# A fused macaron block: its opening in another order, and its last sum in halves

## The chip, the cores and the metric

The kernel runs on one core of a Trainium2 chip. The metric is the device time of one execution in microseconds. Three runs of the kernel before gave 1027.17, 1028.06 and 1028.55 us, median 1028.06 us.

## The reference: what is computed

For x of 8 sequences by 1024 tokens by 128 features, all in float32, three residual steps follow each other:

```python
x = x + 0.5 * _L0_ffn_ref(_layernorm(x, axis=-1), ...)
x = x + _L0_attn_ref(_layernorm(x, axis=-1), L0_attn_w_q, L0_attn_w_k, L0_attn_w_v)
x = x + 0.5 * _L0_ffn_ref(_layernorm(x, axis=-1), ...)
```

The attention is causal, with one head of 128 and rotary positions. The feed-forward step is a mixture of 16 experts of inner width 64, of which a router picks 4 for each token, and one shared expert:

```python
scores = jax.nn.sigmoid(xt.astype(jnp.float32) @ gate_w.T)
_, idx = lax.top_k(scores + gate_b, TOPK)
w = jnp.take_along_axis(scores, idx, axis=-1)
w = w / jnp.sum(w, axis=-1, keepdims=True) * ROUTE_SCALE
comb = zeros.at[token, idx].add(w)
y = sum over experts e of comb[:, e] * (silu_and_mul(xt @ w13[e].T) @ w2[e].T)
y = y + silu_and_mul(xt @ w13_s.T) @ w2_s.T
```

So the router's weight of a token and an expert (`comb`) multiplies that expert's hidden values or its output. It isn't needed for the first product, `xt @ w13[e].T`.

## The kernel before, in words

**Groups.** A group is 512 tokens of one sequence in one of the two feed-forward layers: 2 layers by 8 sequences by 2 halves make 32 groups, in an order written out by hand (the first four sequences' first layer, then the two layers in turn). All 16 experts are computed for every token, as 8 pairs of 128 hidden units, and `comb` zeroes what wasn't picked.

**A group's steps** (class `Group`, L164 to L289). `norm_a` makes the reciprocal deviations: an addition on DVE (L147) and a power on POOL (L148). `norm_b` makes four normalised tiles on DVE (L155). `turn` transposes them on PE (L164) and copies them to `hT` on ACT (L165). `route` is four small products with the router's weights (L188), `score` an exponential on ACT (L194), `top_a`, `top_b` and `top_c` pick the four experts on DVE and make `comb` (L198 to L226). `spread` transposes `comb` on PE (L235), copies it on ACT (L237), writes it to DRAM (`cd`, L239) and reads it back in four DMAs, 512 KB each, so that every partition holds the weights of its expert (`cb`, L245). `up_shared` is the shared expert's product (L254 to L257). `up(k)`, for k from 0 to 7, is the main part: two products of 512 columns on PE (gate L264, up L265), a silu on ACT (L267), the product of the two on DVE (`hidT`, L269) and the multiplication by `cb` on POOL (L270). `down(k)`, for k from 0 to 8, sums the outputs in one bank of PSUM (L276); after k = 8 DVE copies the sum (L279). `add`, run in a slot of the next group, transposes it back (L284), adds it to x on DVE (L287) and for the second layer sends it out (L289).

**What sets the order.** The program is written in the order in which every engine takes its instructions. A group has 18 slots, U0 to U8 around its `up` steps and D0 to D8 around its `down` steps. A table `jobs` says which steps of other groups, of attention and of layer norm statistics stand in which slot; `run(p, slot)` emits them. Products `up(k)` use PSUM banks 2(k%2) and 2(k%2)+1, so an L265 needs the `hidT` product (L269) of two steps earlier to have been read out of its bank.

**The opening.** Group 0 has nobody in front of it. Before its first `up_shared` all its steps from `norm_a` to `spread` stand in one row; then come the statistics of the second half of sequence 0, and on the SP queue the loads of the first half of sequence 1, of the attention's weights, of the rotary table (1 MB), and of the second half of sequence 1. Group 1's `norm_a` stands in slot U1 of group 0, `norm_b` in U2, `turn` in U5, `route` in U6, `score` to `top_c` in D0 to D3, `spread` in D4. In `up(k)` the multiplication by `cb` is emitted right after the product on DVE, so on POOL it stands ahead of what the slot behind it brings, for k = 0 ahead of group 1's L148.

**The queues at the start.** SP's queue loads x (two halves of sequence 0), then the down weights `wd` (512 KB) and `wsd`; ACT's queue loads the router's weights, the shared expert's `ws` and the two halves of the gate and up weights (`wg`, `wu`, 256 KB each). Some of these issues wait for an earlier DMA that used the same semaphore.

Of the kernel before, what the change touches and what calls it, by code (L numbers as in the profile page):

```python
# [11 lines left out]
ALU = mybir.AluOpType  # L12
# [3 lines left out]
P = 128  # L16
# [10 lines left out]
def kernel(  # L27
# [14 lines left out]
    nc = tc.nc  # L42
# [4 lines left out]
    NT = S // P  # L47
    GT = 4
    NG = NT // GT
    W = GT * P  # L50
# [17 lines left out]
    def bank(i, n=1):  # L68
        return psum[:, i * W : (i + n) * W]
# [3 lines left out]
    def other_bank():  # L73
        spare[0] += 1
        return bank(6 + spare[0] % 2)

    def tiles_of(ap):
        return ap.rearrange("p (j q) -> p j q", q=P)

    ident = const.tile([P, P], F32, name="ident")  # L80
# [14 lines left out]
    xs, mvs = [None] * B, {}  # L95

    def load_x(b, g):
        if g == 0:
            xs[b] = xpool.tile([P, NT, D], F32, tag="x", name=f"x{b}")
        tiles = slice(g * GT, (g + 1) * GT)  # L100
        nc.sync.dma_start(
            out=xs[b][:, tiles, :], in_=x[b].rearrange("(t p) d -> p t d", p=P)[:, tiles, :]
        )
# [10 lines left out]
    for n in range(2):  # L114
        cols = slice(n * EI // 2, (n + 1) * EI // 2)
        nc.scalar.dma_start(out=wg[:, cols], in_=w_gate[:, cols])
        nc.scalar.dma_start(out=wu[:, cols], in_=w_up[:, cols])
    load_x(0, 1)
    wd = const.tile([P, NP, D], F32, name="wd")
    nc.sync.dma_start(out=wd, in_=w_down.rearrange("(n p) d -> p n d", p=P))  # L120

# [7 lines left out]
        shared.append(sh)  # L129
    wqkv = const.tile([P, 3, D], F32, name="wqkv")  # L130
    cs = const.tile([P, 2, S], F32, name="cs")

    def stats(key, b, tiles):

        if key not in mvs:
            mvs[key] = small.tile([P, NT, 2], F32, tag="mv", name=f"mv_{key}", bufs=16)
        for t in tiles:
            st = small.tile([P, 6], F32, tag="st", name=f"st_{key}_{t}")  # L140
            nc.vector.bn_stats(st, xs[b][:, t, :])
            nc.vector.bn_aggr(mvs[key][:, t, :], st)
# [26 lines left out]
    class Group:  # L169
# [89 lines left out]
        def up(self, k):  # L259

            nm = f"{self.nm}_{k}"
            units = slice(k * P, (k + 1) * P)
            g_ps, u_ps = bank(2 * (k % 2) + 1), bank(2 * (k % 2))
            nc.tensor.matmul(g_ps, wg[:, units], self.hT, start=True, stop=True)  # L264
            nc.tensor.matmul(u_ps, wu[:, units], self.hT, start=True, stop=True)  # L265
            sg = work.tile([P, W], F32, tag="sg", name=f"sg_{nm}")
            nc.scalar.activation(sg, g_ps, AF.Silu)  # L267
            hid = self.hidT[:, k, :]
            nc.vector.tensor_tensor(hid, u_ps, sg, ALU.mult)  # L269
            nc.gpsimd.tensor_tensor(hid, hid, self.cb[:, k, :], ALU.mult)  # L270

        def down(self, k):
            if k == 0:
                self.y = bank(0)
            w, h = (wd[:, k, :], self.hidT[:, k, :]) if k < NP else (wsd, self.sh)
            nc.tensor.matmul(self.y, w, h, start=(k == 0), stop=(k == NP))  # L276
            if k == NP:
                self.yT = work.tile([P, W], F32, tag="yT", name=f"yT_{self.nm}", bufs=2)
                nc.vector.tensor_copy(self.yT, self.y)  # L279

        def add(self):
            yp = tiles_of(other_bank())
            for j in range(GT):
                nc.tensor.transpose(yp[:, j, :], self.yT[:, j * P : (j + 1) * P], ident)  # L284
            tiles = slice(self.g * GT, (self.g + 1) * GT)
            xg = xs[self.b][:, tiles, :]
            nc.vector.scalar_tensor_tensor(xg, yp, 0.5, xg, ALU.mult, ALU.add)  # L287
            if self.layer == 1:
                nc.sync.dma_start(  # L289
                    out=out[self.b].rearrange("(t p) d -> p t d", p=P)[:, tiles, :], in_=xg  # L290
                )
# [115 lines left out]
    order = [(0, b) for b in range(LAG)]  # L407
    for b in range(LAG, B):
        order += [(1, b - LAG), (0, b)]
    order += [(1, b) for b in range(B - LAG, B)]  # L410
    groups = [
        Group(layer, b, g, 2 * n + g) for n, (layer, b) in enumerate(order) for g in range(NG)
    ]
    NPER = len(groups)
    heads = [Heads(b) for b in range(B)]

    jobs = {}

    def at(p, slot, *fs):
        jobs.setdefault((p, slot), []).extend(fs)  # L420
# [3 lines left out]
    def when(p, slot):  # L424
        return p * len(slots) + slots.index(slot)
# [4 lines left out]
    queue = [(b, i) for b in range(B) for i in range(NT)]  # L430
    starts, done = {}, {}
    for p in range(3, 29):
        for n in range(2 if p in (15, 21) or (p % 2 == 0 and p != 26) else 3):
            if not queue:
# [4 lines left out]
            s, first, e, t0, t1, a = (  # L439
                ((p, "U7"), 4, (p, "D0"), (p, "D3"), (p, "D5"), (p, "D7")),  # L440
                ((p, "D2"), 2, (p, "D5"), (p, "D8"), (p + 1, "U0"), (p + 1, "U2")),
                ((p, "D4"), 4, (p, "D7"), (p + 1, "U3"), (p + 1, "U4"), (p + 1, "U5")),
            )[n]
# [10 lines left out]
    for b in range(B):  # L454
        h, st = heads[b], starts[b]
        ready = when(turn_of[0, b, 1] + 1, "U7")
        if b == 0:
            p0, p1 = st - 1, st - 1
            places = ("U8", "D0", "D2", "D3", "D5", "D6", "D7", "D8")
        else:  # L460
            p0, p1 = st - 2, st - 1
            places = ("D0", "D3", "D5", "D8", "U1", "U3", "U4", "U6")
# [14 lines left out]
    for p, gr in enumerate(groups):  # L477
        steps = (
            gr.norm_a, gr.norm_b, gr.turn, gr.route, gr.score, gr.top_a, gr.top_b, gr.top_c,
            gr.spread,  # L480
        )
        if p == 1:
            places = [(0, s) for s in ("U1", "U2", "U5", "U6", "D0", "D1", "D2", "D3", "D4")]
        else:
            places = [(p - 2, s) for s in ("U5", "D1", "D4", "D6", "D7", "D8", "D8")]
            places += [(p - 1, "U1"), (p - 1, "U3")]
        if p > 0:
            for f, place in zip(steps, places):
                at(*place, f)
        if gr.layer == 1:  # L490
            for t in range(gr.g * GT, (gr.g + 1) * GT):
                assert done[gr.b, t] < when(p - 2, "U5")

        at(p + 1, "U3", gr.add)
        if gr.layer == 0:
            t = gr.g * GT
            for s in ("U5", "U7"):
                at(p + 1, s, lambda b=gr.b, t=t: stats(f"a{b}", b, (t, t + 1)))
                t += 2


    for b in range(2, B):
        p = turn_of[0, b, 0]
        for g in range(NG):
# [2 lines left out]
                p + g - 3, "D6",  # L507
                lambda b=b, g=g: stats(f"f0_{b}", b, range(g * GT, (g + 1) * GT)),
            )
    at(0, "U4", lambda: stats("f0_1", 1, range(GT)))  # L510
    at(0, "D6", lambda: stats("f0_1", 1, range(GT, NT)))

    def load_attention():
        nc.sync.dma_start(out=wqkv, in_=w_qkv)
        nc.sync.dma_start(out=cs, in_=rope)

    def run(p, slot):
        for f in jobs.pop((p, slot), []):
            f()

    gr = groups[0]
# [6 lines left out]
    gr.top_a()  # L528
    gr.top_b()
    gr.top_c()  # L530
    gr.spread()
    stats("f0_0", 0, range(GT, NT))
    load_x(1, 0)
    load_attention()
    load_x(1, 1)
    for p, gr in enumerate(groups):
        gr.up_shared()
        run(p, "U0")
        for k in range(NP):
            gr.up(k)  # L540
            run(p, f"U{k + 1}")
        for k in range(NP + 1):
            gr.down(k)
            run(p, f"D{k}")
    for p in (NPER, NPER + 1):
        for slot in slots:
# [73 lines left out]
```

## Time and profile before

| what | value |
|---|---|
| median of three runs | 1028.06 us |
| the profiled execution's own time | 1027.84 us |
| its span, first to last instruction | 1025.7 us |
| PE, matmuls | 993.1 us busy, 97% of the span |
| DVE / ACT / POOL | 662.5 / 419.7 / 451.9 us busy |
| DMA | 80.20 MB, 78 GB/s on average |
| mean granted PE clock in the records | 0.997 |
| first transpose on PE starts at | 7.42 us |
| first `up` product starts at | 17.14 us |
| last product of group 31 ends at | 1019.26 us |

The chain of waits goes back from the last instruction to the first: at each step to what released it, or to the instruction before it on the same engine. Its columns are the start, the length (both in us) and what it was. The timeline has start, length, engine, line, operation, output and inputs, and in brackets the idle time of the engine ahead of it with what ended it. The table by stage gives busy time of each engine, then the granted PE clock (1.00 is full), the share of DMA engines that were busy, and GB/s. One product in float32 shows as two instructions, so "x2" of L264, L265 or L276 is one product.

### The profile page before, as it was taken

To read this page: it belongs to the slowest core of one execution; us is meant where nothing else is said; L and a number is where in the kernel's file an instruction comes from. 1 tells how busy PE (TensorE), PEld (TensorE's weight loads), DVE (VectorE), ACT (ScalarE), POOL (GpSimd) and SP (SyncE) were. 2 spreads that over 40 slices of the span, in tenths; PEclk is the share of its full clock that TensorE was granted. 3 is DMA by queue.
4 is the path that set the end of the run, shared out by engine and by line. 5 is a ranking of instruction groups with operands and counts; after the bars stand their busy time and mean duration, and the time that the engine had idled before them with its cause. 6 is when DMAs were issued, how large, how long until landed. Compare 5 with 4: busy or idle time off the path is not lost.

```text
span 1025.7 us, 11327 instructions
## 1 busy us (share of the span) xinstructions
PE 993.1 (97%) x3520; PEld 534.2 (52%) x3520; DVE 662.5 (65%) x2032; ACT 419.7 (41%) x734; POOL 451.9 (44%) x382
## 2 busy tenths in 40 slices
PE   5799999999999999999999999999999999999997
PEld 2344455554555455545555555555565555555543
DVE  3566877667775776667677665776657757665542
ACT  2233544443534454434444444443444444343321
POOL 1445734265425562345524464334643355322433
PEclk9999999999999999999999999999999999999999
DMA  5485431354214530345213451234412343124440
GB/s 143 110 173 105 84 67 32 69 104 84 46 39 94 115 81 6 81 94 114 61 23 84 94 114 43 43 82 94 94 42 57 69 94 83 48 58 94 94 93 21
DMA packets 56748, 80.20 MB, mean 78 GB/s; under 512 B 3504, under 2 KB 23280, under 8 KB 56560
## 3 DMA queue, kind: packets, MB, share of 16 engines
q1 hardware_dynamic: 55680, 78.36, 35.5%
q10 hardware_dynamic: 1008, 1.13, 0.3%
q8 instruction: 27, 0.44, 0.2%
q14 instruction: 33, 0.27, 0.1%
HBM read 74.24 MB, written 5.24 MB: 77 GB/s over the span
## 4 chain that ended last, share of the span: by engine, by line
PE 86%; DVE 7%; DMA 2%; issue 2%; ACT 2%; POOL 0%; SPq 0%; ACTq 0%; POOLq 0%; DVEq 0%
PE psum L276 23%; PE psum L265 18%; PE psum L264 17%; PE psum L356 6%; PE psum L395 6%; PE psum L383 3%; PE psum L323 3%; PE psum L188 3%; PE psum L164 2%; PE psum L254 2%; DVE hidT L269 1%; DMA cb<-cd 1%; PE psum L337 1%; DVE sel L220 1%; PE psum L284 1%
## 5 line engine op out<-in xcount | busy, mean ns | idle before, releaser
L270 POOL TENSOR_TENSOR hidT<-hidT,cb 128x512 f32<-128x512 f32 x256 | 324.0, 1270 | 545.2 <-DVE hidT L269 497.3
L265 PE MATMUL psum<-hT,wu 128*128 128x512 f32 x512 | 263.2, 596 | 4.4 <-DVE hidT L269 4.4
L264 PE MATMUL psum<-hT,wg 128*128 128x512 f32 x512 | 263.4, 596 | 0.0
L267 ACT ACTIVATE sg<-psum 128x512 f32<-128x512 f32 x256 | 152.7, 597 | 233.0 <-PE psum L264 217.5
L276 PE MATMUL psum<-hidT,wd 128*128 128x512 f32 x512 | 248.0, 598 | 0.0
L269 DVE TENSOR_TENSOR hidT<-psum,sg 128x512 f32<-128x512 f32 x256 | 175.2, 686 | 100.5 <-PE psum L265 98.4
L265 PEld LDWEIGHTS psum<-hT,wu 128*128 128x128 f32 x512 | 97.7, 191 | 128.2 <-issue 104.2
L276 PEld LDWEIGHTS psum<-hidT,wd 128*128 128x128 f32 x512 | 89.2, 191 | 69.0 <-issue 62.7
L264 PEld LDWEIGHTS psum<-hT,wg 128*128 128x128 f32 x512 | 89.4, 193 | 65.8 <-issue 62.8
L387 ACT COPY prT<-psum 128x512 f32<-128x512 f32 (+2 forms) x64 | 32.4, 506 | 158.6 <-PE psum L383 158.6
L395 PEld LDWEIGHTS psum<-v,prT 128*128 128x128 f32 x576 | 74.4, 192 | 30.6 <-issue 26.5
L395 PE MATMUL psum<-v,prT 128*128 128x128 f32 x576 | 74.6, 275 | 0.0
L356 PE MATMUL psum<-k,q 128*128 128x512 f32 (+2 forms) x192 | 72.4, 486 | 0.0
L399 DVE SCALAR_TENSOR_TENSOR x<-psum,rl,x 128x128 f32<-128x128 f32 x64 | 22.1, 346 | 77.1 <-PE psum L395 70.0
L155 DVE TENSOR_SCALAR xn_f<-x,mv_f,rs_f 128x128 f32<-128x128 f32 x128 | 65.6, 573 | 5.8 <-POOL rs_f L148 5.7
L383 PEld LDWEIGHTS psum<-ident,pr 128*128 128x128 f32 x288 | 36.8, 141 | 49.9 <-issue 42.9
L356 PEld LDWEIGHTS psum<-k,q 128*128 128x128 f32 x192 | 36.6, 190 | 45.8 <-issue 45.1
L362 DVE TENSOR_REDUCE top<-psum 128x1 f32<-128x128 f32 (+3 forms) x64 | 48.5, 758 | 2.2
L383 PE MATMUL psum<-ident,pr 128*128 128x128 f32 x288 | 47.4, 274 | 1.9 <-DVE x L287 1.9
L367 ACT ACTIVATE pr<-psum,top 128x128 f32<-128x128 f32 (+3 forms) x64 | 47.3, 743 | 0.3
L360 DVE TENSOR_TENSOR psum<-psum,causal 128x128 f32<-128x128 f32 x64 | 19.0, 296 | 42.4 <-PE psum L356 42.0
L256 ACT ACT_TABLE_LOAD x31 | 39.8, 1283 | 10.2 <-PE psum L254 10.1
(77 smaller groups left out, 1013.6 us busy)
## 6 DMA issues: line engine op xcount, KB each, us to landing
cb<-cd SPq DMA_DIRECT2D x128, 512.0 KB, 8.5
x<-in_x SPq DMA_DIRECT2D x16, 256.0 KB, 10.9
out_x<-x SPq DMA_DIRECT2D x16, 256.0 KB, 2.4
cd<-cT SPq DMA_DIRECT2D x32, 32.0 KB, 1.8
cs<-in_rope SPq DMA_DIRECT2D x1, 1024.0 KB, 12.4
wd<-in_w_down SPq DMA_DIRECT2D x1, 512.0 KB, 8.1
wg<-in_w_gate ACTq DMA_DIRECT2D x2, 256.0 KB, 7.5
wu<-in_w_up ACTq DMA_DIRECT2D x2, 256.0 KB, 6.4
```

What stands on the lines that cost most here:

```text
L155: nc.vector.tensor_scalar(xn[:, j, :], xs[b][:, t, :], mvs[key][:, t, 0:1], rstd[:, j : j + 1], ALU.subtract, ALU.mult,)
L264: nc.tensor.matmul(g_ps, wg[:, units], self.hT, start=True, stop=True)
L265: nc.tensor.matmul(u_ps, wu[:, units], self.hT, start=True, stop=True)
L267: nc.scalar.activation(sg, g_ps, AF.Silu)
L269: nc.vector.tensor_tensor(hid, u_ps, sg, ALU.mult)
L270: nc.gpsimd.tensor_tensor(hid, hid, self.cb[:, k, :], ALU.mult)
L276: nc.tensor.matmul(self.y, w, h, start=(k == 0), stop=(k == NP))
L356: nc.tensor.matmul(s[:, c:e], h.q[:, i * P : width], h.k[:, c:e], start=True, stop=True)
L362: nc.vector.tensor_reduce(top, s[:, :width], AX.X, ALU.max)
L367: nc.scalar.activation(self.pr[:, : self.width], self.s[:, : self.width], AF.Exp, bias=self.top, scale=SCALE, accum_out=self.h.rl[:, self. ...
L383: nc.tensor.transpose(tp[:, j, :], self.pr[:, (k + j) * P : (k + j + 1) * P], ident)
L395: nc.tensor.matmul(o, self.prT[:, j, :], self.h.v[:, j, :], start=(j == 0), stop=(j == i))
```

## The change

Seven edits, all in the order of emission, in the first group or in the last:

1. Twelve products of the identity with itself, 128 by 128, are put on PE ahead of everything else; their result is overwritten.
2. `load_x(1, 0)`, 256 KB, moves on the SP queue from behind group 0's `spread` to the front of `wd`.
3. Group 0's `spread` moves from ahead of `up_shared` to slot U2, behind `up(1)`. `load_x(1, 1)`, the attention's loads and the statistics of the second half of sequence 0 follow it there; `load_x(1, 1)` now stands ahead of the attention's loads.
4. The multiplication by `cb` becomes a method of its own, `weigh(k)`. It stays where it was, save in group 0: `weigh(0)` is emitted behind `spread` in U2, and `weigh(1)` behind the jobs of U2.
5. Group 1's steps in group 0 move: `norm_a` U1 to U2, `norm_b` U2 to U3, `turn` U5 to U6, `route` U6 to U7, `spread` D4 to D6.
6. Group 2's `norm_a` moves from U5 to U8 of group 0, and the statistics of the first half of sequence 1 from U4 to U7.
7. Group 31's `down` copies its sum in two halves of 256 columns, the first on ACT and the second on DVE, and its `add` becomes `add_last`: two transposes, one addition and one output DMA for each half, the first DMA from ACT's queue, the second from SP's.

On the engines' queues this gives: PE takes the identity products, group 0's transposes and router products, `ws`, `up(0)`, `up(1)`, then the transpose of `comb`. POOL takes `weigh(0)`, then group 1's L148, then `weigh(1)`. DVE takes the choice of experts, then the shared product, the `hidT` products of 0 and 1, the statistics, the L147 addition, `hidT` of 2, the four tiles of `norm_b`, `hidT` of 3. The DMA of `wd` waits for the router's weights to land, which it didn't before. On DVE the second half's copy in group 31 waits for ACT's copy of the first.

```diff
     load_x(0, 1)
+    load_x(1, 0)
     wd = const.tile([P, NP, D], F32, name="wd")
...
+    for n in range(12):
+        nc.tensor.matmul(bank(2)[:, :P], ident, ident, start=True, stop=True)
...
             nc.vector.tensor_tensor(hid, u_ps, sg, ALU.mult)
+
+        def weigh(self, k):
+            hid = self.hidT[:, k, :]
             nc.gpsimd.tensor_tensor(hid, hid, self.cb[:, k, :], ALU.mult)
...
-                nc.vector.tensor_copy(self.yT, self.y)
+                if self.n == NPER - 1:
+                    H = W // 2
+                    nc.scalar.copy(self.yT[:, :H], self.y[:, :H])
+                    nc.vector.tensor_copy(self.yT[:, H:], self.y[:, H:])
+                else:
+                    nc.vector.tensor_copy(self.yT, self.y)
+
+        def add_last(self):
+
+            H = GT // 2
+            for n, queue in enumerate((nc.scalar, nc.sync)):
+                yp = tiles_of(other_bank())[:, :H, :]
+                t = self.g * GT + n * H
+                for j in range(H):
+                    k = n * H + j
+                    nc.tensor.transpose(yp[:, j, :], self.yT[:, k * P : (k + 1) * P], ident)
+                xg = xs[self.b][:, t : t + H, :]
+                nc.vector.scalar_tensor_tensor(xg, yp, 0.5, xg, ALU.mult, ALU.add)
+                queue.dma_start(
+                    out=out[self.b].rearrange("(t p) d -> p t d", p=P)[:, t : t + H, :], in_=xg
+                )
 
         def add(self):
+            if self.n == NPER - 1:
+                return self.add_last()
...
         if p == 1:
-            places = [(0, s) for s in ("U1", "U2", "U5", "U6", "D0", "D1", "D2", "D3", "D4")]
+            places = [(0, s) for s in ("U2", "U3", "U6", "U7", "D0", "D1", "D2", "D3", "D6")]
+        elif p == 2:
+            places = [(0, s) for s in ("U8", "D1", "D4", "D6", "D7", "D8", "D8")]
+            places += [(p - 1, "U1"), (p - 1, "U3")]
...
-    at(0, "U4", lambda: stats("f0_1", 1, range(GT)))
+    at(0, "U7", lambda: stats("f0_1", 1, range(GT)))
...
-    gr.spread()
-    stats("f0_0", 0, range(GT, NT))
-    load_x(1, 0)
-    load_attention()
-    load_x(1, 1)
+
+    jobs[0, "U2"] = [
+        gr.spread, lambda: load_x(1, 1), load_attention,
+        lambda: gr0.weigh(0), lambda: stats("f0_0", 0, range(GT, NT)),
+    ] + jobs.get((0, "U2"), [])
+    gr0 = gr
     for p, gr in enumerate(groups):
         gr.up_shared()
         run(p, "U0")
         for k in range(NP):
             gr.up(k)
-            run(p, f"U{k + 1}")
+            if p == 0 and k < 2:
+                run(p, f"U{k + 1}")
+                if k == 1:
+                    gr.weigh(k)
+            else:
+                gr.weigh(k)
+                run(p, f"U{k + 1}")
```

More of the change, by code (lines that the diff above doesn't have):

```diff
@@ L410 @@
     order += [(1, b) for b in range(B - LAG, B)]
+    NPER = NG * len(order)
     groups = [
@@ L413 @@
     ]
-    NPER = len(groups)
     heads = [Heads(b) for b in range(B)]
```

## The prediction, made blind

> **What bounds the kernel now.** I read the page first: the busy shares, the 40 slices and the chain's summary.
>
> ```profile
> span 1025.7 us, 11327 instructions
> PE 993.1 (97%) x3520; PEld 534.2 (52%) x3520; DVE 662.5 (65%) x2032; ACT 419.7 (41%) x734; POOL 451.9 (44%) x382
> PE   5799999999999999999999999999999999999997
> PE 86%; DVE 7%; DMA 2%; issue 2%; ACT 2%; POOL 0%; SPq 0%; ACTq 0%; POOLq 0%; DVEq 0%
> ```
>
> PE is full in every slice but the first two and the last. The edits touch only these, so a microsecond won in the first group is handed on by a stream that PE sets. Next, the chain in order of time, 0 to 60 us:
>
> ```profile
> 15.96 1.78 DMA cd<-cT
> ...
> 18.44 6.84 DMA cb<-cd
> ...
> 25.45 1.27 POOL hidT L270
> 26.71 0.98 POOL rs_f L148
> ...
> 28.92 0.85 DVE xn_f L155 x3
> 29.76 0.61 DVE hidT L269
> 30.37 0.04 issue
> 30.42 1.83 PE psum L265 x2
> ```
>
> PE stands still from about 26.7 to 30.42. The reason isn't that it lacks `cb`: POOL's first multiplication waits for `cb`, group 1's L148 is queued behind it, DVE's four tiles of `norm_b` (L155) wait for L148, the third `hidT` product is queued behind them, and PE's fifth L265 needs that product's bank. The timeline shows a second stop, 2.29 us, for `comb` of group 1, and what happens when POOL has work in store while DVE runs the four tiles:
>
> ```profile
> 46.29 0.30 PE L235 MATMUL psum<-ident,comb 128*64 128x128 f32 x1 [2.29 <-DVE comb L226]
> ...
> 124.31 3.73 POOL L270 TENSOR_TENSOR hidT<-hidT,cb 128x512 f32<-128x512 f32 x3
> 124.47 3.91 DVE L155 TENSOR_SCALAR xn_f<-x,mv_f,rs_f 128x128 f32<-128x128 f32 x4
> ```
>
> The same four tiles take 1.11 us at 7.02 where POOL is idle, 2.05 us at 27.72 beside one multiplication, and 3.91 us here beside three. The table by stage shows PE's clock:
>
> ```profile
> 20.46:30.70 10.24, 6.51 (x16) 2.76 (x15) 4.44 (x9) 2.39 (x4) 3.73 (x4) 1.00 1.09 223
> 30.70:34.10 3.40, 3.40 (x8) 1.77 (x8) 2.48 (x11) 0.58 (x1) 2.95 (x3) 0.50 0.97 366
> ```
>
> After the stop the clock is half for 3.4 us. Records begin at 20.46, yet the products between 15.4 and 20.46 start 1.71 us apart (17.14, 18.85) and later ones 0.86 (21.37, 22.23): PE starts at half speed too. Last, the chain's end:
>
> ```profile
> 1019.29 0.70 DVE yT L279
> ...
> 1020.03 0.67 PE psum L284 x4
> ...
> 1020.73 0.69 DVE x L287
> ```
>
> [...] raised 5.2 us after PE's steady work began (15.22 to 20.46), dropped at 30.70, raised again 3.4 us later. [...]
>
> **The change, part by part.**
>
> *Identity products.* Not in the trace; nearest are plain 128-column products at 0.107 us per instruction (L395: 6% of the span by 576 instructions), so 0.213 at half clock: 12 x 2 x 0.213 = 5.1 us from about 1.45 (the identity is ready at 1.40) to 6.6, ahead of the first transpose at 7.42. They cost nothing there; below nothing only through the clock. [...] I take a raised clock.
>
> *Up to `comb`.* At full clock the last transpose ends 0.2 us sooner (8.66 to 8.45), and the eight router instructions take 0.96 (row of 35.22) and not 1.89: `score` starts at 10.09 for 11.27, `comb` is done 1.18 sooner at 13.99. Meanwhile PE does what was behind it: five products (`ws`, two pairs) of 0.86, from 9.90 to 14.20. So `comb` is transposed at 14.20 and not 15.22; behind ACT's silu of pair 1 the copy ends at 14.80, and `cd` starts at 14.82 for 15.96: 1.14 sooner.
>
> *Weights.* Now `ws` is needed at 9.9, the first `wg` at 10.8, `wu` at 11.6. They landed at 8.8, 9.7 and 10.3 (issue plus landing in the DMA list). The 256 KB put in front lie on SP's queue, which was full of `wd` until 9.9 anyway; `wd` goes later, needed after 37. I take nothing; if the margin of 1.1 us breaks, up to 1 us of a PE that has to stop anyway.
>
> *The first stop.* With `cd` 1.14 sooner, `weigh(0)` runs at 24.31, L148 ends at 26.54. The knot is the same: L148 is still behind `weigh(0)`, and the move to U3 puts one more `hidT` in front of `norm_b`. PE therefore gets one pair further (through the sixth L264, at 20.6) and stops at the sixth L265. But now `weigh(1)` and `weigh(2)` are both ready, so two of the four tiles wait for POOL: the first ends at 27.86, the second 1.22 later, the others at 29.6; `hidT` 3 at 30.2. PE resumes at 30.25 for 30.42: the 1.14 is almost eaten by the second wait. The gain is the pair's 2 products: left over are five products, a set of transposes and the router, 5 x 0.86 + 0.43 + 0.80 = 5.5 us, plus 1.9 for the half clock (3.4 to 3.9 us of it) = 7.4[...]. The first `down` starts at 37.8 for 39.55: 1.75.
>
> *The second stop.* The chain to `comb` of group 1 runs from the last silu over the 1.28 us table load to `score`, then waits for POOL's last multiplication. All shift by about 1.8: `comb` at 44.4 for 46.24, group 2's tiles at 42.6 for 44.4. L148 of group 2, now behind `weigh(7)`, ends at 41.05, before its tiles start at 41.45. PE reaches these transposes after five `down` products (37.8 + 4.3 = 42.1): stops 0.5. It reaches `comb` after two more, 44.75: no stop. So 0.5 for 2.3, about 2.0 with the pipelines' overlaps (47.4 for 51.20 at the next `up_shared`, 3.8 in all). The statistics moved to U7 (1.6 us) end before the last `hidT` can start (37.8); POOL's backlog in group 1, with `cb` 2.2 us later against that group, is worked off before its `down` (weigh 5 at 63.3 for a need at 67). Cover gone, it would cost 0.3.
>
> *The end.* ACT's half copy 0.37 and DVE's 0.42 (rows of 128x256 below), in a row since DVE waits for ACT; two transposes 0.40; the half addition about 0.46, between 0.35 (L399, 128 columns) and 0.69 (512).
>
> ```profile
> L387 ACT COPY prT<-psum 128x256 f32<-128x256 f32 x8 | 3.0, 372 | 13.8 <-PE psum L383 13.8
> L389 DVE COPY prT<-psum 128x256 f32<-128x256 f32 x8 | 3.4, 423 | 4.2 <-PE psum L383 4.1
> ```
>
> The second copy ends at 1020.12, its transposes at 1020.56, its addition at 1021.05 for 1021.42: 0.37. The last DMA has half the bytes: the old one moved for 1.3 us and landed after 3.2, so 0 to 0.65 more. I take 0.35, 0.7 in all.
>
> Sum: 3.8 + 0.7 = 4.5. The profiled execution had span 1025.7 and 1027.84 in all, 2.1 around: 1021.2 and 1023.3. The median, 0.22 above it, goes to 1023.6.
>
> **Rivals.**
>
> *The clock isn't raised by the identity products* (that edit does nothing). Then the router ends at 11.24 as before, and five products at up to 1.71 stand ahead of `comb`. With the rise 5.2 us after 9.34, as before, `comb` is transposed at 17.2, 3.0 later: gain 1.5, 1026.5. [...]
>
> *Slower: PE stays at half clock through all five products.* Then `comb` is transposed at 19.8, 5.6 later than I forecast, and the whole chain to 30.25 with it: 4.5 - 5.6 = 1.1 lost, 1029.2. It decides for a loss if the clock rises after about 17.7 (a transpose after 18.7). Against it: both rises seen came within 5.3 us of steady work.
>
> [...] PE resumes 1.25 sooner, with the end at its better bound 1.6 in all: 1022.0. [...] against it 3.91 us.
>
> **How the numbers follow.** Forecast 0.62; no rise 0.20; the better case 0.11; the slower 0.07. About 0.2%, 2 us, is what a measurement of this kernel can tell from no change: faster is under 1026.0. The forecast, the better case and a third of the second count as faster: 0.62 + 0.11 + 0.06, taken down to 0.77 for what I haven't seen; same 0.17, slower 0.06. The range runs from 1021.8, just under the better case, to 1026.8, the second case with a rise 0.6 us later.
>
> **What would show it.** Right: clock records from about 5 to 7 us and router instructions of 1 us; `comb` transposed near 14.2; a stop of PE from 20.6 to about 30.2 on `hidT`, with the four L155 tiles at about 3 us; next stop about 0.5, on L155 and not on `comb`; group 31's last addition 1.8 us after its last product (2.15 before). Wrong: 1.7 us products before `comb`, a wait on `wg` or `wu`, or PE not stopping at 20.6.

## The result, and the profile after

Nine runs of the changed kernel gave a median of 1025.21 us (1022.95 to 1027.64), nine of the kernel before 1028.09 us: 2.9 us less, a ratio of 0.9973 with a 95% interval of 0.9963 to 0.9984. It is faster, by less than the 4.5 us that were forecast; the time lies inside the range. The runs follow the mean granted clock of PE: 0.995 in the shortest, 0.989 in the longest. The profiled execution took 1025.43 us, its span 1023.6. The page of the kernel after:

```profile
span 1023.6 us, 11380 instructions
PE 996.8 (97%) x3544; PEld 536.8 (52%) x3544; DVE 664.3 (65%) x2033; ACT 420.4 (41%) x735; POOL 452.0 (44%) x382
PE   7799999999999999999999999999999999999998
PEclk9799999999999999999999999999999999999999
PE 89%; DVE 6%; issue 2%; ACT 2%; DMA 1%; POOL 0%; SPq 0%; ACTq 0%; POOLq 0%; DVEq 0%
```

Only the first two slices and the last have changed, as the edits would have it. PE's 24 new instructions are the identity products, in the first. In the second slice, 25.6 to 51.2 us, the granted clock is 7 tenths where it was 9 before: PE is just as busy, but slower. The same row of the kernel before:

```profile
PEclk9999999999999999999999999999999999999999
```

The chain in order of time, kernel after:

```profile
16.95 1.80 DMA cd<-cT
...
19.45 7.32 DMA cb<-cd
26.93 1.26 POOL hidT L278
28.19 0.98 POOL rs_f L153
...
30.39 1.81 DVE xn_f L160 x3
32.21 0.61 DVE hidT L274
```

The chain has the same members as before (the lines have new numbers: L270 is now L278, L148 is L153, L155 is L160, L269 is L274, L265 is L270), but `cd` starts 1.0 us later than before, not 1.1 sooner, and what hangs on it comes later too: `weigh(0)` by 1.5 us, PE by 2.4. The timeline of the kernel after, DVE's tiles and PE's stop:

```profile
29.20 3.01 DVE L160 TENSOR_SCALAR xn_f<-x,mv_f,rs_f 128x128 f32<-128x128 f32 x4 [9.48 <-POOL rs_f L153]
...
32.86 2.08 PE L270 MATMUL psum<-hT,wu 128*128 128x512 f32 x2 [10.22 <-DVE hidT L274]
```

PE stands still from 22.64 to 32.86, on the wait that was forecast, and the tiles take the 3 us that were forecast beside two multiplications. The reason for the delay is in the table by stage of the kernel after (start:end, length, busy us and instructions of PE, PEld, DVE, ACT and POOL, granted clock, DMA share, GB/s). The records of the clock begin at 4.35, so the first row's 1.00 stands for no record; the identity products there start 0.213 us apart, and 0.112 us apart from 4.38 on (two to a product).

```profile
0.94:4.35 3.41, 2.89 (x13) 2.89 (x14) 0.27 (x1) 0.00 (x0) 1.87 (x9) 1.00 0.56 146
4.35:7.77 3.42, 1.59 (x14) 1.37 (x12) 2.04 (x12) 1.28 (x1) 1.02 (x1) 1.00 0.89 259
7.77:11.18 3.41, 2.73 (x14) 1.80 (x14) 0.96 (x5) 1.28 (x3) 0.00 (x0) 1.00 1.00 314
11.18:14.59 3.41, 3.41 (x5) 1.33 (x4) 3.03 (x21) 2.00 (x3) 0.00 (x0) 0.50 0.02 5
32.86:38.49 5.63, 5.63 (x10) 2.93 (x11) 1.23 (x2) 1.18 (x2) 3.76 (x3) 0.50 0.21 89
```

The clock rose at 4.35, fell back at 11.18 for one step of 3.41 us, and after the stop stayed at half for 5.63 us and not for 3.4. What the profiled executions show at each step, in us (the forecast's last two rows are 1019.26 - 3.8 and 6.44 - 0.7):

| step | before | after | forecast |
|---|---|---|---|
| `comb` of group 0 transposed on PE | 15.22 | 16.35 | 14.20 |
| first multiplication by `cb` (`weigh(0)`) | 25.45 | 26.93 | 24.31 |
| PE resumes after the first stop | 30.42 | 32.86 | 30.25 |
| first `down` | 39.55 | 41.35 | 37.8 |
| group 1's `up_shared` | 51.20 | 50.91 | 47.4 |
| last product of group 31 ends | 1019.26 | 1018.80 | 1015.5 |
| last product's end to the end of the span | 6.44 | 4.80 | 5.7 |

So in these two executions, of 2.1 us of span, 0.46 came from the opening and 1.64 from the end. By far the larger part had been expected of the opening.

### The profile page after: what moved, and what is told of

Its sections match the earlier page's. It is cut to its first block, busy times and chain, and to the rows that moved or that the text cites. A ratio compares the mean times of both kernels' runs of the same rounds, so it can differ in the third digit from the quotient of the medians.

```text
span 1023.6 us, 11380 instructions
## 1 busy us (share of the span) xinstructions
PE 996.8 (97%) x3544; PEld 536.8 (52%) x3544; DVE 664.3 (65%) x2033; ACT 420.4 (41%) x735; POOL 452.0 (44%) x382
## 4 chain that ended last, share of the span: by engine, by line
PE 89%; DVE 6%; issue 2%; ACT 2%; DMA 1%; POOL 0%; SPq 0%; ACTq 0%; POOLq 0%; DVEq 0%
PE psum L284 24%; PE psum L270 19%; PE psum L269 18%; PE psum L386 6%; PE psum L425 6%; PE psum L413 3%; PE psum L353 3%; PE psum L193 3%; PE psum L259 2%; PE psum L169 2%; DVE hidT L274 1%; PE psum L367 1%; DVE sel L225 1%; PE psum L314 1%; DMA cb<-cd 1%
## 5 line engine op out<-in xcount | busy, mean ns | idle before, releaser
L278 POOL TENSOR_TENSOR hidT<-hidT,cb 128x512 f32<-128x512 f32 x256 | 324.2, 1271 | 544.6 <-DVE hidT L274 494.3
L270 PE MATMUL psum<-hT,wu 128*128 128x512 f32 x512 | 264.0, 597 | 10.9 <-DVE hidT L274 10.9
L269 PE MATMUL psum<-hT,wg 128*128 128x512 f32 x512 | 263.6, 597 | 0.0
L274 DVE TENSOR_TENSOR hidT<-psum,sg 128x512 f32<-128x512 f32 x256 | 175.3, 686 | 98.5 <-PE psum L270 95.5
L270 PEld LDWEIGHTS psum<-hT,wu 128*128 128x128 f32 x512 | 97.9, 192 | 135.1 <-issue 104.9
L269 PEld LDWEIGHTS psum<-hT,wg 128*128 128x128 f32 x512 | 89.0, 192 | 65.2 <-issue 61.9
L160 DVE TENSOR_SCALAR xn_f<-x,mv_f,rs_f 128x128 f32<-128x128 f32 x128 | 67.6, 588 | 10.7 <-POOL rs_f L153 10.7
L413 PE MATMUL psum<-ident,pr 128*128 128x128 f32 x288 | 47.4, 274 | 1.9 <-DVE x L317 1.9
L397 ACT ACTIVATE pr<-psum,top 128x128 f32<-128x128 f32 (+3 forms) x64 | 47.4, 744 | 0.3
```

Of the source, the lines that this page charges most:

```text
L160: nc.vector.tensor_scalar(xn[:, j, :], xs[b][:, t, :], mvs[key][:, t, 0:1], rstd[:, j : j + 1], ALU.subtract, ALU.mult,)
L397: nc.scalar.activation(self.pr[:, : self.width], self.s[:, : self.width], AF.Exp, bias=self.top, scale=SCALE, accum_out=self.h.rl[:, self. ...
L413: nc.tensor.transpose(tp[:, j, :], self.pr[:, (k + j) * P : (k + j + 1) * P], ident)
```

## The experiments

Ratios are to the kernel before on the same chip. Experiments differ from the kernel after unless the text says "before".

### The end by itself

Before, with the seventh edit and nothing else.

```diff
-                nc.vector.tensor_copy(self.yT, self.y)
+                if self.n == NPER - 1:
+                    H = W // 2
+                    nc.scalar.copy(self.yT[:, :H], self.y[:, :H])
+                    nc.vector.tensor_copy(self.yT[:, H:], self.y[:, H:])
+                else:
+                    nc.vector.tensor_copy(self.yT, self.y)
...
+        def add_last(self):
```

> The kernel before with the last sum in halves and nothing else (edit 7). Theory A, from the traces of before and after: from the last product's end to the span's end it was 6.44 us before and 4.80 after, so this edit alone is worth 1.6 us: 1026.4 us, with the last DMA landing about 1.9 us after its issue. Rival B, the prediction's term: 0.7 us, 1027.4 us, the long landing of before (3.2 us) having been a straggler that comes in some executions of either kernel.

Measured: 1026.67 us against 1029.32, ratio 0.9975 [0.9965, 0.9986], 2.6 us faster (1.4 to 3.6). Its profile has the opening of before (the last product ends at 1019.56 for 1019.26); from there to the end it takes 4.8 us for 6.44. The end is worth more than the 0.7 that I gave it.

### The kernel after with the old end, and the kernel after once more

The first undoes the seventh edit, the second is unchanged.

```diff
-                if self.n == NPER - 1:
-                    H = W // 2
-                    nc.scalar.copy(self.yT[:, :H], self.y[:, :H])
-                    nc.vector.tensor_copy(self.yT[:, H:], self.y[:, H:])
-                else:
-                    nc.vector.tensor_copy(self.yT, self.y)
+                nc.vector.tensor_copy(self.yT, self.y)
...
-            if self.n == NPER - 1:
-                return self.add_last()
```

> The kernel after with the last sum as before (edit 7 undone): one copy, four transposes, one addition, one DMA of 256 KB. Theory A: the halves are worth 1.6 to 2.6 us, of which only 0.35 us is the additions; the rest is the landing of the last DMA, 3.2 us for one of 256 KB and 1.9 us for two of 128 KB: this run is 1.6 us or more slower than after on the same chip, and its span ends about 6.4 us after the last product (4.8 after). Rival B: the long landing was one engine's straggler in that one execution; then the span ends about 5.4 us after the last product and the run is 0.6 us slower than after.

> The kernel after itself, to stand on the same chip as its neighbours. Both theories: a ratio to before between 0.9963 and 0.9984, runs spread over 3 to 5 us with the share of half clock[...].

Measured side by side: with the old end 1026.70 us, ratio 0.9981 [0.9974, 0.9989], so the opening alone gives 2.0 us (1.1 to 2.7); the kernel after 1025.76 us, ratio 0.9972 [0.9961, 0.9982]. The end's share here is 0.9 us by the medians, and the two intervals overlap. The old end's profile needs 6.2 us from the last product on, the other 4.81: the profiles agree on 1.4 to 1.6 for the end, and the timed 2.6 and 0.9 lie on both sides of it. How the 2.9 us divide between opening and end is thus known only roughly: one pair of profiles gives 0.5 and 1.6, these runs 2.0 and 0.9.

### Where the end's time is: the last DMA

The timeline gives 1.82 us from the last product to the last addition, where it was 2.16: 0.34 sooner. The other 1.3 us lie in the last DMA. The DMA view of the kernel after, from 1020.0 to the end (queues with packets, MB and share of 16 engines; then issues with KB and us to landing):

```profile
q10 hardware_dynamic: 272, 0.13, 13.1%
q1 hardware_dynamic: 272, 0.13, 12.6%
...
out_x<-x ACTq DMA_DIRECT2D x1, 128.0 KB, 1.9
out_x<-x SPq DMA_DIRECT2D x1, 128.0 KB, 1.9
```

The same view of the kernel before, from 1021.3 to 1026 us, with its GB/s in 40 equal slices:

```profile
GB/s 0 0 0 0 0 0 0 0 4 209 301 275 279 275 349 266 205 48 9 9 9 4 22 22 17 0 0 0 0 0 0 0 0 0 0 0 0 0 0 0
...
q14 instruction: 1, 0.01, 0.4%
...
out_x<-x SPq DMA_DIRECT2D x1, 256.0 KB, 3.2
```

Is 1.9 us for 3.2 the price of half the bytes? Before, with one whole addition, and its output sent in two DMAs at the same moment:

```diff
+            if self.n == NPER - 1:
+                H = GT // 2
+                for n, queue in enumerate((nc.scalar, nc.sync)):
+                    t = self.g * GT + n * H
+                    queue.dma_start(
+                        out=out[self.b].rearrange("(t p) d -> p t d", p=P)[:, t : t + H, :],
+                        in_=xg[:, n * H : (n + 1) * H, :],
+                    )
-            if self.layer == 1:
+            elif self.layer == 1:
```

> The kernel before, with only the last output DMA divided in two of 128 KB on two queues; copies, transposes and the addition stay whole. Theory A: the larger part of what edit 7 brings is the landing, not the additions: last addition 2.15 us after the last product as before, landing near 1.9 us, the span's end 5.1 us after the last product (6.44 before, 4.80 after): 1.2 us less than before. Rival B: the landing was long for another reason than the size (one packet of another kind stood among the DMA's packets): landing 2.3 us or more, gain 0.5 us or less.

Measured: 1028.04 us, ratio 0.9999 [0.9991, 1.0007]; 6.1 us from the last product on. The same view of that experiment, from 1021.3 to the end:

```profile
q14 instruction: 1, 0.01, 0.6%
...
out_x<-x SPq DMA_DIRECT2D x1, 128.0 KB, 2.7
out_x<-x ACTq DMA_DIRECT2D x1, 128.0 KB, 2.8
```

Halves of 128 KB land after 2.7 and 2.8 us: dividing the DMA doesn't bring the 1.9. But here both halves move at the same moment, so the bytes in flight are those of before, and this run doesn't price them. The earlier outputs do. Before, `out_x` leaves in sixteen DMAs of 256 KB, all issued by L289. The view of that line:

```profile
DMA to landing us min/median/max: 2.3/2.4/3.2
```

Fifteen of them land after 2.3 or 2.4 us, and only the last after 3.2. So of the 1.3 us, 0.5 are the bytes (2.4 to 1.9) and 0.8 are something else. What the last DMA has and those fifteen haven't is one packet of another queue in the midst of the transfer, of q14, which the view names `instruction`; behind it the stream of before falls from over 200 GB/s to between 4 and 22 for its last 0.8 us. Over all fourteen profiles, the 183 DMAs of 256 KB of `out_x` with no packet of an `instruction` queue beside them (from 0.9 us after the issue to the landing) landed after 2.3 or 2.4 us, the 29 with one after 2.4 to 4.6, five of them after 2.4. Such a packet stands in the last DMA in all three profiles with a whole last addition (before, the old end, this one: last landing after 3.2, 2.9 and 2.8 us) and in none of the eleven with halves (1.8 to 1.9). Why it stands there in the three and not in the eleven wasn't shown: no run moved it alone.

### Without the identity products

```diff
-    for n in range(12):
-        nc.tensor.matmul(bank(2)[:, :P], ident, ident, start=True, stop=True)
```

> The kernel after without the twelve identity products (edit 1 undone). Theory A: the early rise of the clock is worth something even though it falls back at 11 us, since the transposes, the router and the shared product run at full clock; without it the transpose of comb comes at about 17.5 to 18 us (16.35 after) and the whole is 1 to 1.5 us slower than after: 1026.5 us. Rival B: since the clock falls back before the pairs, the products buy nothing: 1025.2 us, comb transposed within 0.3 us of after's 16.35.

Measured: 1025.73 us, ratio 0.9962 [0.9949, 0.9976]. As that came out no slower than the kernel after, it was taken again on another chip:

> The kernel after without identity products, a second time, for another profile: the first one's time was 0.9962 of before, no slower than after, although its comb was transposed 1.7 us later. Theory A: what the twelve products save ahead of comb is given back after the long stop[...] (half clock for 5.6 us after the stop in the kernel after). Then comb comes at 16.5 to 18 us here, and the half clock after the stop is 3.5 to 4.5 us in the typical execution. Rival B: the first result was chance: this one is 0.998 of before.

Measured: 1026.39 us, ratio 0.9976 [0.9967, 0.9986]. The two lie on both sides of the 0.9973 and 0.9972 of the kernel after: twelve identity products alone bought nothing that can be measured. In both profiles the clock rises only at 16.1 to 16.3, and `comb` is transposed at 18.01 and 17.84, 1.5 to 1.7 us later than after; group 1's `up_shared` starts at 52.46 and 52.25, 1.3 to 1.6 later. The medians don't show this. Both profiled executions had a lower mean clock (0.992) than most of the timed runs (0.994 to 0.995), so they may overstate the loss: 0.995 for 0.992 over some 1009 us of records is about 6 us less of half clock, by estimate. Where it is given back isn't settled.

### More identity products, so that the clock stays

Sixteen in front, and three between group 0's transposes and its router, where PE waits for ACT's copy.

```diff
-    for n in range(12):
+    for n in range(16):
...
     gr.turn()
+    for n in range(3):
+        nc.tensor.matmul(bank(2)[:, :P], ident, ident, start=True, stop=True)
     gr.route()
```

> The kernel after with 16 instead of 12 identity products at the start and 3 more between group 0's transposes and its router products, in a wait of PE of 0.7 us. Theory A: the clock fell back at 11.2 us [...]; with the gaps filled it stays full through the pairs, comb is transposed near 14.5 us (16.35 after) and the time is about 1.7 us lower, 1023.5 us, with no half clock in the records between the first rise and the long stop. Rival B: [...] it falls back all the same: 1025.2 us, or 0.6 us more where the added products run at half clock ahead of the router.

Measured: 1022.61 us, ratio 0.9931 [0.9918, 0.9943], 7.1 us faster than before (5.9 to 8.4). Its timeline, PE:

```profile
14.40 0.27 PE L240 MATMUL psum<-ident,comb 128*64 128x128 f32 x1
...
30.45 2.08 PE L270 MATMUL psum<-hT,wu 128*128 128x512 f32 x2 [9.43 <-DVE hidT L274]
...
37.79 4.45 PE L284 MATMUL psum<-hidT,wd 128*128 128x512 f32 x10
...
47.34 1.02 PE L259 MATMUL psum<-hT,ws 128*128 128x512 f32 x2
```

These are the forecast's 14.20, 30.25, 37.8 and 47.4, within 0.2 us. The clock stayed up from 6.43 to 23.5, inside the stop, and PE worked at half clock from 30.45 to 33.74, 3.3 us. The last product ends 3.77 us sooner than before (3.8 forecast). So the steps behind the clock were right, and the clock was the one that failed. The profiles differ by 5.4 us, 3.8 here and 1.6 at the end; the timed 7.1 is against a kernel before that was slower on this chip (median 1029.32) than on the others (1028.09 to 1028.57).

The three in the gap alone, with the twelve in front as they are:

```diff
     gr.turn()
+    for n in range(3):
+        nc.tensor.matmul(bank(2)[:, :P], ident, ident, start=True, stop=True)
     gr.route()
```

> The kernel after with its 12 identity products and 3 more between group 0's transposes and its router products. It tells which of the two additions of the earlier run with 16 and 3 kept the clock. Theory A: [...] the three in the gap keep the clock: about 4 us faster than after, 1.0 us or less slower than with 16 and 3. Rival B: [...] about half of the runs stay near after's time and the median lies 1 to 3 us above that with 16 and 3.

Measured: 1023.62 us, ratio 0.9947 [0.9931, 0.9964]; its interval meets that of the sixteen and three, and just that of the kernel after. In its profile `comb` is transposed at 14.42: the clock was kept. The nearest rise without the three is that of the power first (below): there the clock rose at 5.25 and fell at 8.66, here it rose at 5.08 and stayed. (The rest is less good than with sixteen and three: `cb` took 0.6 us longer, the half clock after the stop 4.7 us, and group 1's `up_shared` starts at 48.70.) The four profiles with twelve products and without the three (the kernel after, once more, with the old end, and with the power first, below) fell back, at 11.18, 11.03, 8.95 and 8.66; the five with the three, four of which have sixteen in front, kept the clock until PE stopped for something else.

### The moved load of x

The sixteen and three, with `load_x(1, 0)` back behind `spread`.

```diff
-    load_x(1, 0)
...
-        gr.spread, lambda: load_x(1, 1), load_attention,
+        gr.spread, lambda: load_x(1, 0), load_attention, lambda: load_x(1, 1),
```

> The kernel after with 16 and 3 identity products, and the load of the first half of sequence 1 back behind spread (edit 2 undone; the order of the later loads as before). The prediction took nothing for this edit. Theory A: the same time within 0.5 us of the run with 16 and 3 alone (0.9931 of before). Rival B: with the load in front, the first half of sequence 0 landed 0.16 us later (4.08 for 3.92) and cb took 0.5 us longer, so undoing it gains 0.5 us or more.

Measured: 1023.07 us, ratio 0.9947 [0.9934, 0.9959] beside 0.9931 [0.9918, 0.9943]. Undoing the edit gains nothing; it is worth nothing or a little. I had taken nothing.

### Which wait PE's long stop is

Group 1's statistics and `norm_a`, with its power on POOL, ahead of `weigh(0)`; the identity products are those of the kernel after.

```diff
-        lambda: gr0.weigh(0), lambda: stats("f0_0", 0, range(GT, NT)),
-    ] + jobs.get((0, "U2"), [])
+        lambda: stats("f0_0", 0, range(GT, NT)),
+    ] + jobs.get((0, "U2"), []) + [lambda: gr0.weigh(0)]
```

> The kernel after with group 1's power (L153, norm_a) and its statistics emitted ahead of the first multiplication by cb on POOL, and nothing else changed. Theory A, the knot: PE's long stop (22.5 to 32.9 us) is due to the power queued behind that multiplication, not to a lack of cb; with the power ahead the tiles of norm_b come at about 20 us, PE goes through all eight pairs and reaches the first down product at about 28 us (41.4 after); then POOL, one multiplication each 1.27 us from 27 us, sets the pace, and the next group's shared product starts at about 44 us (50.9 after): 1025.2 - 6.9 = 1018.3 us. Rival B: the stop only moves to the first down product, which needs cb anyway[...]: the next group starts no earlier than 50 us and the time is 1024 to 1026 us.

Measured: 1018.85 us, ratio 0.9901 [0.9885, 0.9917], 10.2 us faster than before (8.5 to 11.8). In its profile `weigh(0)` starts at 27.78, 0.9 later than in the kernel after, and yet PE runs on: the first `down` starts at 29.28 for 41.35, although the clock was half for 6.83 us here (8.66 to 15.49). The stop hung on POOL's order, not on `cb`. The next one does too. Its timeline:

```profile
38.09 1.01 POOL L153 TENSOR_TENSOR rs_f<-rs_f,neg_half 128x4 f32<-128x4 f32 x1
39.13 1.11 DVE L160 TENSOR_SCALAR xn_f<-x,mv_f,rs_f 128x128 f32<-128x128 f32 x4 [5.75 <-POOL rs_f L153]
39.53 1.24 PE L169 MATMUL psum<-ident,xn_f 128*128 128x128 f32 x4 [3.88 <-DVE xn_f L160]
```

Group 2's power stands behind all eight multiplications, and DVE and PE wait for it: part of what the first stop gave is lost here. The same order with sixteen and three:

```diff
-    for n in range(12):
+    for n in range(16):
...
+    for n in range(3):
+        nc.tensor.matmul(bank(2)[:, :P], ident, ident, start=True, stop=True)
...
+        lambda: stats("f0_0", 0, range(GT, NT)),
+    ] + jobs.get((0, "U2"), []) + [lambda: gr0.weigh(0)]
```

> The kernel after with group 1's power ahead of the first multiplication by cb, and with 16 and 3 identity products. Theory A: the two gains are of different stretches (comb transposed at 14.4 us and not 16 to 17.5; no stop on the power), so they add: about 3.2 us below the run with the power first alone, 13 us below before, the next group's shared product at about 43 us. Rival B: POOL's multiplications set the pace either way and cb's way through DRAM is the limit; the gain over the power first alone is under 1 us.

Measured: 1017.88 us, ratio 0.9900 [0.9880, 0.9920]. The profile is 3.2 us further at group 1's `up_shared` (42.92 for 46.12), but the intervals, from two chips, are the same: that the clock adds to this order isn't shown.

### Both powers ahead

The sixteen and three; `weigh(0)` to `weigh(4)` together behind U5, group 2's `norm_a` back in U5, its statistics in U4, and its `norm_b` in U6 instead of D1.

```diff
-            places = [(0, s) for s in ("U8", "D1", "D4", "D6", "D7", "D8", "D8")]
+            places = [(0, s) for s in ("U5", "U6", "D4", "D6", "D7", "D8", "D8")]
...
-    at(0, "U7", lambda: stats("f0_1", 1, range(GT)))
+    at(0, "U4", lambda: stats("f0_1", 1, range(GT)))
...
-        lambda: gr0.weigh(0), lambda: stats("f0_0", 0, range(GT, NT)),
+        lambda: stats("f0_0", 0, range(GT, NT)),
...
-            if p == 0 and k < 2:
+            if p == 0 and k < 5:
                 run(p, f"U{k + 1}")
-                if k == 1:
-                    gr.weigh(k)
+                if k == 4:
+                    for m in range(5):
+                        gr.weigh(m)
```

> As the run with the power first and 16 and 3 identity products, and group 2's statistics, power and normalised tiles too are brought ahead (its tiles behind the sixth pair), all first five multiplications by cb being emitted behind both powers. In the earlier run PE's last stop (32.0 to 35.9 us) was on group 2's tiles, whose power stood behind POOL's eighth multiplication. Theory A: that stop goes, what is left is POOL's pace of 1.27 us a multiplication from 24.5 us on, and the next group's shared product starts at about 37.5 us (42.9): 5 us less, about 1012.5 us. Rival B: DVE's choice of experts for group 1[...] takes the place of the tiles: at most 2 us less.

Measured: 1012.69 us (1012.58 to 1012.96), ratio 0.9847 [0.9834, 0.9860]: 15.7 us faster than before (14.4 to 17.1), and the fastest of all. After its rise at 4.54 the clock stays full to the end of the span, and its four runs lie within 0.4 us of each other, where the nine of the kernel after spread over 4.7. One short stop is left. Its timeline:

```profile
24.08 4.12 DVE L160 TENSOR_SCALAR xn_f<-x,mv_f,rs_f 128x128 f32<-128x128 f32 x4 [0.53 <-POOL rs_f L153]
24.40 9.97 POOL L278 TENSOR_TENSOR hidT<-hidT,cb 128x512 f32<-128x512 f32 x8 [0.36 <-DMA cb<-cd]
28.12 1.27 DVE L274 TENSOR_TENSOR hidT<-psum,sg 128x512 f32<-128x512 f32 x2
28.90 4.53 PE L284 MATMUL psum<-hidT,wd 128*128 128x512 f32 x10 [2.23 <-POOL hidT L278]
```

POOL works through eight multiplications without a pause, DVE's four tiles take 4.12 us beside it, and the last two `hidT` products, queued behind them on DVE, come late. The view names POOL for PE's wait, but the multiplication that the first `down` needs was done at 25.7; what ended just before 28.90 is the first of these two products, and `down` sums in the PSUM bank that this product must first have read.

## Why the prediction was right and wrong

**Right: the direction, and what holds the opening.** PE's stop lay on POOL's queue: `weigh(0)` waits for `cb`, group 1's power stands behind it, DVE's tiles behind that. Emitting the power first removed the stop with `cb` no sooner.

**Failed: "I take a raised clock".** The clock was raised, at 4.35, while the identity products ran, but it wasn't kept. The sign that I had named for being wrong, 1.7 us products before `comb`, came: two start at 11.26 and 12.96, 1.70 apart. That the clock would rise was an assumption, which no trace of the kernel before showed for such products; and I asked only whether it would rise, not whether it would still be up at `comb`. PE idles 1.83 us between the last of them and the transposes, and 0.68 us before the router; at 11.18 the clock fell for 3.41 us, amid the five products that stand ahead of `comb`. Half a clock over 3.41 us is 1.7 of the 2.15 us by which `comb` came later than forecast; the rest of them wasn't taken apart. In the profile of the old end, which has the same opening, it stayed down longer, 6.83 us (8.95 to 15.78), and `comb` was transposed at 17.71. Another 0.5 came from `cb`: from the start of `cd` to `weigh(0)` it took 9.98 us, and I had carried over 9.49 from before. The first rival priced almost this loss (1026.5), but by a rise that doesn't come at all. With sixteen products in front and three in the gap the whole path from `comb` to group 1's `up_shared` is the one on record.

**Failed with it: 3.4 to 3.9 us of half clock after the stop.** It was 5.63. The 3.4 are those of the kernel before; the 0.5 on top, and the 0.15 that I put on the sum of 7.4 (30.25 to 37.8), were an estimate of mine that no trace showed. The stop's end is tied by the chain over `comb` and `cb` to the time at which PE got its clock: in the five profiles with a rise on the way to `comb` (after, after again, old end, and the two without identity products) PE resumes 17.9 to 18.3 us after that rise, and the half clock lasts 5.6 to 6.0 us in each. In the records of the kernels before and after, the levels up to 38.5 us last 3.41, 6.83, 10.24 and 13.65 us, which is 1 to 4 times 3.41; the 13.65 are this half clock, which began at 24.83, inside the stop, and ended at 38.48. What sets its length wasn't shown. The price is 1.0 us: 2.6 late at the stop's end, 3.6 at the first `down`.

**Right: the first stop's members and the tiles.** PE stopped on `hidT`, at its sixth L270, and from the end of the power through the tiles (3.01 us) to that product it took 3.69 us (3.71 forecast). No product waited for its weights, and the moved load cost nothing. The rival in which PE resumes 1.25 us sooner falls: POOL's two multiplications (29.13 to 31.61) ran on without a gap, the two tiles beside them took 1.27 and 1.30 us, and the two behind them, with POOL idle, 0.34 each. In "Both powers ahead" the four took 4.12 us beside eight multiplications.

**Right: the second stop.** From the first `down` to group 1's `up_shared` it took 9.56 us (9.6 forecast), where it was 11.65. This is the opening's one gain that came in full: 2.1 us. The 1.80 us by which the first `down` is late take most of it.

**Wrong in size: the end.** The copies and additions gave 0.34 (0.37 forecast). The DMA's landing gave 1.3 where I took 0.35, with 0 to 0.65 as bounds that I read from the bytes alone. For the bytes that was near: they gave 0.5. The other 0.8 I had put at nothing: I took the 3.2 us of the one last DMA for the price of 256 KB, where the median of the sixteen is 2.4, and the rest went with a packet of another queue that I hadn't looked for. By the profiles, 0.9 us too little here hid part of the 3.3 that were missing at the last product. That was luck: without it the time would be about 1026.1, still inside the range, whose upper end lay at the first rival, but 2.5 us above the forecast and not 1.6.

**The slower rival** (half clock through all five products) didn't come: in the kernel after's profile the clock fell for 3.41 us, and in that of the old end for 6.83; in both the last two of the five ran at full clock.

Open are what decides whether the clock stays up, and where the kernel without identity products gets its time back.

## What to carry to other kernels

A clock raised by filler is worth something only if it is still up when the real work comes: follow it through the gaps behind the filler, and fill those (here it rose at 4.35 and fell at 11.18, ahead of `comb` at 16.35; with three products in the 0.68 us in front of the router it was still up at `comb`). Before pricing an edit to a wait, ask what stands in the queue behind the waiting instruction: here a power of 1 us behind a multiplication that waited for a DMA held PE for ten, and emitting it first took the gain from 2.9 to 10.2 us. One DMA's landing isn't the price of its bytes: compare it first with the others of its size (here 3.2 us with fifteen of 2.3 or 2.4), and look for a packet of another queue beside it.

## What the runs showed of the hardware

In these profiles PE's recorded busy time over the 3.41 us ahead didn't tell whether the clock stayed up. Behind 1.59 us of 3.42 it stayed (identity products, then transposes; kernel after, 4.35 to 7.77), and behind 2.73 of 3.41 it fell (transposes, the router's products of 16 columns, the first of `ws`; 7.77 to 11.18). Of two stretches that hold nearly the same work, it stayed behind the one with 2.17 of 3.41 (three in the gap, 5.08 to 8.49) and fell behind the one with 2.04 (power first, 5.25 to 8.66). Whether the kind of work counts wasn't shown: no run here varied the kind alone.

A packet of an `instruction` queue beside an output DMA of 256 KB went with a landing after 2.4 to 4.6 us, where it was 2.3 or 2.4 without one (29 and 183 DMAs). After the last landing the span went on for some 1.1 us in the kernel before as in the kernel after (1024.65 to 1025.7, 1022.55 to 1023.6), so there a longer landing was a longer span.
